# A four-layer graph kernel on one core: a low-bit check of the adjacency, a branch ahead of layer 3, and float32r halves behind it

## The chip, the core and the metric

The kernel runs on one core of a Trainium2 chip. Its metric is the device time in microseconds (us); lower is better. Three timed executions gave 1043.35, 1043.86 and 1045.03 us, so the median is 1043.86 us. One more execution was taken with the hardware profiler, and every row below comes from it.

Four engines of the core compute: TensorE (PE in the profile; its weight loads are PEld), VectorE (DVE), ScalarE (ACT) and GpSimd (POOL). The queues of SyncE (SP), ACT and POOL issue transfers.

## The reference, cut to what matters

The inputs are x (2708 nodes x 128 features), adj (2708 x 2708, zeros and ones with a full diagonal) and small weights. Four layers follow each other, each of the form x = x + layer(relu(layernorm(x))):

- Layer 0: attention over adj with a row sum.
- Layer 1: adj plus the identity, scaled on both sides by the root of its degrees, times the features, times a weight, relu.
- Layer 2: adj transposed times the features, divided by degrees, two weights, a batch norm over all nodes, relu.
- Layer 3, where the change lies:

```python
XW = jnp.matmul(X, W)
s_col = jnp.matmul(XW, a[0, :f])
s_row = jnp.matmul(XW, a[0, f:])
Z1 = jax.nn.leaky_relu(s_row[:, None] + s_col[None, :], negative_slope=0.01)
den = jnp.exp(Z1)
num = jnp.matmul(A, den)
att = jnp.where(num != 0, den / jnp.where(num != 0, num, 1.0), 0.0)
H = jnp.matmul(A, jnp.matmul(att, XW))
```

A and den are both 2708 x 2708, so `num` alone would be a product of 2708 x 2708 x 2708.

## The kernel before, in words

The nodes are cut into T = 22 tiles of 128 (the last has 20 rows), and the 2708 columns of a result into NB = 6 blocks: five of 512 and one of 148 (`E0`). All operands of the large products are float32. A product (`product`, `aggregate`) streams one tile of adjacency rows (128 x 2708, 1354 KB) after the other from HBM, uses the tile as the moving operand for all six blocks, and sums into six PSUM accumulators; the last four tiles are taken block by block, so that each block can be finished (`finish1`, `finish2`, `finish3`) while the next is summed. In layer 2 the loads go through `load_with_turn`; three tiles of adj are kept in SBUF from layer 0 (`kept`), the others come through seven stream buffers.

Layer 3 avoids the cubic product. It ranks the nodes by their row score and cuts them into chunks of CH = 126 nodes in that order (`CH = P - 2`, `NC` = 22 chunks). The exponential of a leaky relu has two branches. For a column node, all chunks but one lie wholly on one branch, so their share of `num` is a sum that is formed once per chunk (`sums`, `wts`): two rows per chunk, kept in HBM as `pre_d`. Only the chunk in which the change of branch falls has to be multiplied out. The column nodes are sorted into NE = 22 steps of 128 such that each step needs at most two chunks (NS = 44 half steps). For a half step, `fetch` gathers the CH adjacency rows of the chunk into a tile of 128 rows by an indirect transfer on the POOL queue, and a second gather puts the two rows of `pre_d` into the partitions behind them. The matching stationary operand `dmat[:, s, :]` (128 x 128) is made by `densities`. Lines 933 to 941 move the finished chunk sums from PSUM through `hn` to `pre_d`.

The loop of layer 3 (lines 965 to 992) does, for each of the 22 steps s:

- the gathers of the two half steps (four buffers `rows`, in pool `steps`) and of the step's feature rows (`fetch_xw`), on POOL;
- `e` = max(row_a + c_rel, 0) on DVE (line 975);
- for each of six blocks a PSUM bank `num` that gets two products, one per half step (line 980), then its logarithm on ACT into `ln` (line 984). There are two such banks;
- three subtractions e - ln on DVE (line 986) and the exponential of the whole `e` on ACT (line 988). Each logarithm and exponential stage is preceded by a load of ACT's function table;
- `spread_values(s - 1)`: six products of the step before with its `e` as the moving operand (line 962), summed over all steps in six accumulators.

The products of the loop are pinned in the order in which they are written: the `num` products of step s, then the values of step s - 1, then the `num` products of step s + 1.

After the loop the accumulators are turned and scaled into `hn` (lines 997 to 1002), and a last product (lines 1026 to 1028) streams the 22 tiles of adj_t again through SP's queue, with `hn` as the stationary operand; the streaming buffers are the four of `steps` and three of `late`. `finish3` turns a finished block, adds it to x and stores it.

Of the kernel before, what the change touches and what calls it, by code (L numbers as in the profile page):

```python
# [8 lines left out]
F32 = mybir.dt.float32  # L9
BF16 = mybir.dt.bfloat16  # L10
I32 = mybir.dt.int32
AF = mybir.ActivationFunctionType
# [5 lines left out]
def kernel(  # L18
# [19 lines left out]
    nc = tc.nc  # L38
# [23 lines left out]
    def fill(a, src, t):  # L62

        if rows(t) < P:
            nc.gpsimd.memset(a, 0.0)
        nc.sync.dma_start(a[: rows(t), :], src[t * P : t * P + rows(t), :])
        return a
# [138 lines left out]
    def aggregate(stationary, moving, accs, start, stop, blocks=range(NB)):  # L206
        for b in blocks:
            lo, hi = E0[b]
            nc.tensor.matmul(accs[b][:, : hi - lo], stationary, moving[:, lo:hi], start=start, stop=stop)  # L209
# [13 lines left out]
    with ExitStack() as stack:  # L223
# [168 lines left out]

        def load_with_turn(t):
            a = kept[t] if t in kept else load_rows(adj, t)
            if t not in kept and turns:
                b = turns.pop(0)
                p = bank()
                turned(p, h2, TILES[b])
                nc.vector.tensor_copy(hT[:, spans(b)], p[:, : len(TILES[b]) * P])
            return a  # L400
# [11 lines left out]
        product(order2, lambda t: h2[:, t, :], load_with_turn, range(NB), finish2)  # L412
        nc.vector.bn_aggr(tot[:, 0:2], st2)
# [15 lines left out]
    CH = P - 2  # L429
# [6 lines left out]
    pre_d = dram.tile([2 * NC, N], F32, name="pre_d")  # L436
# [4 lines left out]
    def stream_rows(src, t):  # L441
        pool = pools[0]
        pools.append(pools.pop(0))
        return fill(pool.tile([P, N], F32, tag="rows", name="rows"), src, t)
# [9 lines left out]
    r_exp = keepers.tile([P, T], F32, name="r_exp")  # L454

    def gather(out, src, idx):
# [5 lines left out]
        )  # L462

# [3 lines left out]
    with tc.tile_pool(name="tab", bufs=1) as tab, tc.tile_pool(name="tabs", bufs=2) as tabs:  # L467
# [27 lines left out]
        nc.vector.memset(first[0:1, :], 1.0)  # L495
        slope_hi = const.tile([P, 1], F32, name="slope_hi")
        nc.vector.tensor_scalar(slope_hi, part, float(CH), -0.99, ALU.is_equal, ALU.mult)
        nc.vector.tensor_scalar_add(slope_hi, slope_hi, 1.0)
        slope_lo = const.tile([P, 1], F32, name="slope_lo")
        nc.vector.tensor_scalar(slope_lo, part, float(CH + 1), 0.99, ALU.is_equal, ALU.mult)  # L500
        nc.vector.tensor_scalar_add(slope_lo, slope_lo, 0.01)
# [425 lines left out]
        for s0 in range(0, FIRST, 4):  # L927
            densities(s0)
        for t in range(NEARLY, T):
            sums(t)  # L930
        for s0 in range(FIRST, NS, 4):
            densities(s0)
        pre_sb = hn.rearrange("p t d -> p (t d)")[:, : 3 * BW].rearrange("p (b i) -> p b i", i=BW)
        with tc.high_priority():
            for b in range(3):
                w = BLK[b][1] - BLK[b][0]
                nc.scalar.copy(pre_sb[: 2 * NC, b, :w], accs[b][: 2 * NC, :w])
                nc.vector.tensor_copy(pre_sb[64 : 64 + 2 * NC, b, :w], accs[b][64 : 64 + 2 * NC, :w])
            flat = hn.rearrange("p t d -> p (t d)")
            for h, queue in enumerate((nc.sync, nc.scalar)):  # L940
                queue.dma_start(pre_d[:, h * HALF : (h + 1) * HALF], flat[64 * h : 64 * h + 2 * NC, :HALF])

    with tc.tile_pool(name="att", bufs=2) as attp:

        accs = [acc_bank(b) for b in range(NB)]
        done = {}

        def fetch(s):
            if s < 2:
                a = first_rows[s][:, :N]  # L950
            else:
                a = steps.tile([P, N], F32, tag="rows", name="rows")
                one = gather(a[:CH, :], adj_t[:, :], row_i[:CH, s : s + 1])
                if s < 6:
                    tc.keep_in_program_order(one)
            gather(a[CH:, :], pre_d[:, :], pre_i[0:2, s : s + 1])
            return a
# [7 lines left out]
        for s in range(NE):  # L965
            a2 = [fetch(2 * s + h) for h in range(2)]
            if s >= 3:
                fetch_xw(s)
            xw = xw_s[s % 4]
            m = nc.vector.tensor_scalar_mul(xw, xw, c_exp[:, s : s + 1])  # L970
            if s < 4:
                tc.keep_in_program_order(m)
            e = attp.tile([P, N], F32, tag="e", name="e")
            ln = attp.tile([P, N], F32, tag="ln", name="ln")
            nc.vector.tensor_scalar(e, row_a[:, :N], c_rel[:, s : s + 1], 0.0, ALU.add, ALU.max)  # L975
            beg = 0
            for b, (lo, hi) in enumerate(E0):
                num = bank()
                for h in range(2):
                    m = nc.tensor.matmul(  # L980
                        num[:, : hi - lo], dmat[:, 2 * s + h, :], a2[h][:, lo:hi], start=(h == 0), stop=(h == 1)
                    )
                    tc.keep_in_program_order(m)
                nc.scalar.activation(ln[:, lo:hi], num[:, : hi - lo], AF.Ln, bias=tiny)  # L984
                if b in (2, 4, 5):
                    nc.vector.tensor_sub(e[:, beg:hi], e[:, beg:hi], ln[:, beg:hi])  # L986
                    beg = hi
            nc.scalar.activation(e, e, AF.Exp)
            done[s] = (xw, e)
            if s:  # L990
                spread_values(s - 1)
        spread_values(NE - 1)


    scale = small.tile([P, T], F32, tag="scale", name="scale")
    nc.vector.scalar_tensor_tensor(scale, deg, 0.0, r_exp, ALU.not_equal, ALU.mult)
    for b in range(NB):
        evacuate(b, yT, accs[b])
        p = bank()
        turned(p, yT, TILES[b], True)  # L1000
        for q, t in enumerate(TILES[b]):
            nc.vector.tensor_scalar_mul(hn[:, t, :], p[:, cols(q)], scale[:, t : t + 1])


    late = ctx.enter_context(tc.tile_pool(name="late", bufs=3))
    pools = [steps] * 4 + [late] * 3

    def finish3(b, acc):
        evacuate(b, yT, acc)
        p = bank()  # L1010
        turned(p, yT, TILES[b], True)
        t0 = TILES[b][0]
        f = len([t for t in TILES[b] if t < TF])
        nc.vector.tensor_add(
            xs[:, t0 : t0 + f, :].rearrange("p t d -> p (t d)"),
            xs[:, t0 : t0 + f, :].rearrange("p t d -> p (t d)"),
            p[:, : f * P],
        )
        nc.sync.dma_start(
            out[t0 * P : (t0 + f) * P, :].rearrange("(t p) d -> p t d", p=P), xs[:, t0 : t0 + f, :]  # L1020
        )
        if f < len(TILES[b]):
            nc.vector.tensor_add(xs[:TAIL, TF, :], xs[:TAIL, TF, :], p[:TAIL, cols(f)])
            nc.sync.dma_start(out[TF * P :, :], xs[:TAIL, TF, :])

    product(
        list(range(T)), lambda t: hn[:, t, :], lambda t: stream_rows(adj_t, t), range(NB), finish3
    )
# [32 lines left out]
```

## Time and profile before

| what | value |
|---|---|
| median of three timed executions | 1043.86 us |
| the profiled execution: its own time | 1046.11 us |
| the profiled execution: span | 1044.3 us |
| PE busy, share of the span | 956.5 us, 92% |
| DVE, ACT, POOL busy | 461.3, 440.4, 165.3 us |
| mean granted TensorE clock | 0.972 |
| first product of the layer 3 loop to last product of the kernel | 613.7 to 1039.0 us |
| bytes moved | 213.06 MB, mean 204 GB/s |

How to read it: a float32 product on 128 columns of weights shows as two MATMUL records (and two weight loads). A group's row gives the line, the engine, the operation, the tiles written and read, the count, the busy time and the mean duration of one. Matmuls are pipelined: durations of neighbours overlap, so the pace is read from the busy time of a run of them. The idle time in a row is that of the engine just before the group, with what ended it. The profiled execution took 1.8 us more than its span and 2.25 us more than the median.

### The profile page before, as it was taken

How to read it: one execution, taken by the hardware profiler on the slowest of the kernel's cores; microseconds unless marked ns; L12 is line 12 of the kernel's file. 1: busy time of each engine (PE TensorE's matmuls, PEld its weight loads, DVE VectorE, ACT ScalarE, POOL GpSimd, SP SyncE). 2: the span in 40 equal slices, each digit the busy share in tenths (PEclk: the TensorE clock that was granted, in tenths of full speed). 3: DMA queues.
4: the chain of work that ended last, by engine and by line, in shares of the span. 5: the costliest groups of instructions: out<-in, count | busy, mean ns of one | idle time of the engine just before them, and what ended most of it. 6: DMA issues, size and time to landing. Idle time of an engine off the chain costs nothing.

```text
span 1044.3 us, 8022 instructions
## 1 busy us (share of the span) xinstructions
PE 956.5 (92%) x2850; PEld 426.0 (41%) x2850; DVE 461.3 (44%) x869; ACT 440.4 (42%) x579; POOL 165.3 (16%) x156
## 2 busy tenths in 40 slices
PE   4699999999999999966697768999999999999998
PEld 3333333344454544442232123444444444444444
DVE  5799889660004100269787242333333333340002
ACT  4579775230005000168402665665656666640000
POOL 3000001020002000020002041444334443200000
PEclk9899999999999999988899889999999999999999
DMA  8257445258865683074069744655556655569841
GB/s 300 94 213 266 175 165 192 55 225 310 309 229 205 221 302 123 0 320 162 1 257 360 198 163 177 218 192 187 183 200 218 216 181 193 198 249 369 312 170 53
DMA packets 36426, 213.06 MB, mean 204 GB/s; under 512 B 8043, under 2 KB 16923, under 8 KB 17363
## 3 DMA queue, kind: packets, MB, share of 16 engines
q1 hardware_dynamic: 21223, 146.96, 38.0%
q0 software_dynamic: 9152, 62.46, 17.0%
q10 hardware_dynamic: 6011, 3.14, 1.2%
q8 instruction: 22, 0.36, 0.1%
q14 instruction: 18, 0.14, 0.0%
HBM read 209.23 MB, written 3.32 MB: 204 GB/s over the span
## 4 chain that ended last, share of the span: by engine, by line
PE 77%; DVE 9%; ACT 7%; DMA 3%; issue 2%; POOL 1%; ACTq 0%; DVEq 0%; POOLq 0%
PE acc L209 37%; PE bank L980 16%; PE acc L962 10%; PE bank L301 7%; ACT L984 3%; DMA rows<-in_adj_t_dram 2%; PE acc L640 2%; ACT ln L984 1%; POOL rstd L160 1%; DVE bits L577 1%; PE bank L185 1%; DVE st L171 1%; ACT row_a L580 1%; PE bank L917 1%; PE acc L252 1%
## 5 line engine op out<-in xcount | busy, mean ns | idle before, releaser
L980 PE MATMUL bank<-rows,dflat 128*128 128x512 f32 x504 | 201.7, 550 | 10.6 <-ACT ln L984 10.6
L980 PEld LDWEIGHTS bank<-rows,dflat 128*128 128x128 f32 x504 | 90.6, 191 | 119.7 <-issue 91.5
L986 DVE TENSOR_TENSOR e<-e,ln 128x1536 f32<-128x1536 f32 (+2 forms) x66 | 70.5, 1097 | 145.3 <-ACT ln L984 145.3
L984 ACT ACTIVATE ln<-bank,tiny 128x512 f32<-128x512 f32 x132 | 79.4, 634 | 83.4 <-PE bank L980 83.2
L962 PE MATMUL acc<-e,xw 128*128 128x512 f32 (+1 forms) x264 | 103.4, 542 | 0.0
L209 PE MATMUL acc<-rows,hn 128*128 128x512 f32 (+1 forms) x264 | 101.7, 542 | 0.0
L209 PE MATMUL acc<-a,hn 128*128 128x512 f32 (+1 forms) x264 | 100.9, 542 | 0.0
L209 PE MATMUL acc<-a,hs 128*128 128x512 f32 (+1 forms) x228 | 88.1, 542 | 0.0
L286 ACT ACTIVATE tau<-row_a,e_neg,e_lo 128x1536 f32<-128x1536 f32 (+1 forms) x44 | 65.0, 1509 | 37.3 <-PE bank L301 27.4
L204 ACT COPY yT<-acc 128x512 f32<-128x512 f32 x9 | 5.2, 581 | 178.4 <-PE acc L209 174.9
L301 PE MATMUL bank<-tau,pick 128*6 128x512 f32 x180 | 72.6, 542 | 0.0
L962 PEld LDWEIGHTS acc<-e,xw 128*128 128x128 f32 x264 | 48.7, 190 | 52.6 <-issue 47.6
L209 PEld LDWEIGHTS acc<-a,hn 128*128 128x128 f32 x264 | 47.0, 190 | 50.2 <-issue 50.0
L209 PEld LDWEIGHTS acc<-rows,hn 128*128 128x128 f32 x264 | 46.8, 190 | 49.0 <-issue 48.8
L457 POOL DMA_INDIRECT rows<-in_adj_t_dram,row_i x42 | 41.9, 998 | 154.2 <-PE bank L980 147.8
L209 PE MATMUL acc<-yT,hs 128*128 128x512 f32 x132 | 57.6, 574 | 7.8 <-DVE yT L292 7.8
L289 DVE SCALAR_TENSOR_TENSOR tau<-tau,e_hi,a 128x1536 f32<-128x1536 f32 (+1 forms) x38 | 60.5, 1623 | 3.0 <-ACT tau L286 3.0
L975 DVE TENSOR_SCALAR e<-row_a,c_rel 128x2708 f32<-128x2708 f32 x22 | 35.8, 1630 | 57.3 <-PE acc L962 57.2
L209 PEld LDWEIGHTS acc<-a,hs 128*128 128x128 f32 x228 | 41.2, 190 | 45.4 <-issue 45.4
L640 PE MATMUL acc<-rows,wts 128*44 128x452 f32 (+1 forms) x216 | 49.3, 568 | 9.5 <-DMA rows<-in_adj_t_dram 9.4
L457 POOL DMA_INDIRECT xw<-xw_d,xw_i x22 | 41.2, 1873 | 93.7 <-DVE xw_i L841 87.3
L209 PE MATMUL acc<-row_b,hs 128*128 128x512 f32 x132 | 55.5, 553 | 0.0
(343 smaller groups left out, 1048.9 us busy)
## 6 DMA issues: line engine op xcount, KB each, us to landing
a<-in_adj_dram SPq DMA_DIRECT2D x38, 1354.0 KB, 6.5
rows<-in_adj_t_dram SPq DMA_DIRECT2D x38, 1354.0 KB, 7.2
a<-in_adj_t_dram SPq DMA_DIRECT2D x21, 1354.0 KB, 5.8
keep<-in_adj_dram SPq DMA_DIRECT2D x2, 1354.0 KB, 5.8
dflat<-in_adj_t_dram SPq DMA_DIRECT2D x2, 1354.0 KB
xw_d<-hs ACTq DMA_DIRECT2D x1, 1408.0 KB
row_a<-rdeg_d ACTq DMA_DIRECT2D x1, 1354.0 KB
yT<-in_adj_t_dram SPq DMA_DIRECT2D x1, 1354.0 KB, 5.6
```

The costliest lines, as they stand in the source:

```text
L160: nc.gpsimd.tensor_tensor(dst, s[:, :n], neg_half[:, :n], ALU.pow)
L209: nc.tensor.matmul(accs[b][:, : hi - lo], stationary, moving[:, lo:hi], start=start, stop=stop)
L286: nc.scalar.activation(tau[:, :w], row_a[:, h0:h1], AF.Relu, bias=e_neg[:, t : t + 1], scale=e_lo[:, t : t + 1])
L289: nc.vector.scalar_tensor_tensor(tau[:, :w], tau[:, :w], e_hi[:, t : t + 1], a[:, h0:h1], ALU.add, ALU.mult)
L301: nc.tensor.matmul(den[: len(E0), : hi - lo], pick[:, b, :], tau[:, lo - h0 : hi - h0], start=(ndone == 0), stop=(t == T - 1 and b == NB - 1),
L457: return nc.gpsimd.indirect_dma_start(out=out, out_offset=None, in_=src, in_offset=bass.IndirectOffsetOnAxis(ap=idx, axis=0),)
L640: nc.tensor.matmul(accs[b][64 * h : 64 * h + 2 * NC, : hi - lo], wts[:, t, :], a[:, lo:hi], start=(t == 0), stop=(t == T - 1),)
L962: m = nc.tensor.matmul(accs[b][:, : hi - lo], xw, e[:, lo:hi], start=(s == 0), stop=(s == NE - 1))
L975: nc.vector.tensor_scalar(e, row_a[:, :N], c_rel[:, s : s + 1], 0.0, ALU.add, ALU.max)
L980: m = nc.tensor.matmul(num[:, : hi - lo], dmat[:, 2 * s + h, :], a2[h][:, lo:hi], start=(h == 0), stop=(h == 1))
L984: nc.scalar.activation(ln[:, lo:hi], num[:, : hi - lo], AF.Ln, bias=tiny)
L986: nc.vector.tensor_sub(e[:, beg:hi], e[:, beg:hi], ln[:, beg:hi])
```

## The change

The change reads the adjacency once for its low bits, sets a flag, and puts the layer 3 loop and the last product behind a branch on that flag. If any adjacency entry has a bit among its twelve lowest, the old float32 arithmetic runs (`rest(False, ...)`). Otherwise `rest(True, ...)` runs, in which the adjacency tiles and gathered rows are of type float32r, and the other operand of each product is cut into a high and a low float32r half, each of which is multiplied once with the tile.

- Layer 2: for each of the 22 adj tiles, DVE masks the low twelve bits into `yT` or `row_b` and ACT sums them into a column of `low`. The first checks wait until the fourth streamed tile; then up to two are made per loaded tile.
- Ahead of the layer 3 loop: `low` is reduced, summed by a 1 x 1 product and compared; the result is the integer `flag`. The chunk size goes from 126 to 124 nodes (22 chunks still), because each gathered tile now takes four rows of `pre_d`: the two sums, cut into high and low halves. `pre_d` has 88 rows instead of 44, written by four transfers instead of two, after a mask and a subtraction per block on DVE.
- The gathers of the first four half steps (steps 0 and 1) stay ahead of the branch and in float32; steps 0 and 1 use the old products.
- In the exact arm, steps 2 to 21 gather into float32r tiles, DVE makes `d_hi` and `d_lo` from the step's two stationary operands, and each block has four products instead of two. `ln` has one buffer instead of two.
- After the loop, DVE makes `y_hi` and `y_lo` (128 x 22 x 128 each) from `hn`. The last product streams float32r tiles, and `fill` issues these loads on POOL's queue instead of SP's. `late` has one buffer instead of three.
- The transfers into float32r tiles read float32 from HBM, so they change the type on the way.

```diff
     def fill(a, src, t):
         if rows(t) < P:
-            nc.gpsimd.memset(a, 0.0)
-        nc.sync.dma_start(a[: rows(t), :], src[t * P : t * P + rows(t), :])
+            nc.gpsimd.memset(a if a.dtype == F32 else a.bitcast(F32), 0.0)
+        queue = nc.sync if a.dtype == F32 else nc.gpsimd
+        queue.dma_start(a[: rows(t), :], src[t * P : t * P + rows(t), :])
...
     def aggregate(stationary, moving, accs, start, stop, blocks=range(NB)):
+        parts = stationary if isinstance(stationary, list) else [stationary]
         for b in blocks:
             lo, hi = E0[b]
-            nc.tensor.matmul(accs[b][:, : hi - lo], stationary, moving[:, lo:hi], start=start, stop=stop)
+            for i, w in enumerate(parts):
+                nc.tensor.matmul(accs[b][:, : hi - lo], w, moving[:, lo:hi],
+                    start=start and i == 0, stop=stop and i == len(parts) - 1)
...
+        low = const.tile([P, T], F32, name="low")
+        nc.gpsimd.memset(low, 0.0)
+        unchecked = []
+        def low_bits(t, a):
+            junk = (yT, row_b)[t % 2][:, :N]
+            bits = junk.bitcast(I32)
+            m = nc.vector.tensor_scalar(bits, a.bitcast(I32), 0xFFF, None, ALU.bitwise_and)
+            n = nc.scalar.activation(junk, bits, AF.Identity, accum_out=low[:, t : t + 1])
...
         def load_with_turn(t):
             a = kept[t] if t in kept else load_rows(adj, t)
+            unchecked.append((t, a))
+            if 3 <= t < TF - 2 or t == TF:
+                for _ in range(min(2, len(unchecked))):
+                    low_bits(*unchecked.pop(0))
...
-    CH = P - 2
+    CH = P - 4
...
-    pre_d = dram.tile([2 * NC, N], F32, name="pre_d")
+    pre_d = dram.tile([4 * NC, N], F32, name="pre_d")
...
+    def high_bits(dst, src):
+        nc.vector.tensor_scalar(dst.bitcast(I32), src.bitcast(I32), -4096, None, ALU.bitwise_and)
...
+        low_all = tab.tile([P, 1], F32, name="low_all")
+        nc.vector.tensor_reduce(low_all, low, AX.X, ALU.add)
+        p = acc_bank(4)
+        nc.tensor.matmul(p[:1, :1], low_all, ones[:, 0:1], start=True, stop=True)
+        flag_f = tab.tile([1, 1], F32, name="flag_f")
+        nc.vector.tensor_scalar(flag_f, p[:1, :1], 0.0, None, ALU.is_gt)
+        nc.vector.tensor_copy(flag, flag_f)
...
             for b in range(3):
...
+                high_bits(pre_hi[:w, lo:hi], flat[:w, lo:hi])
+                nc.vector.tensor_sub(pre_lo[:w, lo:hi], flat[:w, lo:hi], pre_hi[:w, lo:hi])
+            for o, part_sb in ((0, pre_hi), (2 * NC, pre_lo)):
+                for h, queue in enumerate((nc.sync, nc.scalar)):
+                    queue.dma_start(
+                        pre_d[o : o + 2 * NC, h * HALF : (h + 1) * HALF], part_sb[64 * h : 64 * h + 2 * NC, :HALF]
+                    )
...
+    for s in range(4):
+        ahead[s] = fetch(s)
+    def rest(exact, stack3):
...
+            for s in range(NE):
+                short = exact and s >= 2
+                a2 = [rows_of.pop(2 * s + h, None) or fetch(2 * s + h, F32R if short else F32) for h in range(2)]
...
+                if short:
+                    d_hi = attp.tile([P, 2, P], F32R, tag="d_hi", name="d_hi")
+                    d_lo = attp.tile([P, 2, P], F32R, tag="d_lo", name="d_lo")
+                    nc.vector.tensor_copy(d_hi, d2)
+                    nc.vector.tensor_sub(d_lo, d2, d_hi)
+                    terms = [(d[:, h, :], a2[h]) for h in range(2) for d in (d_hi, d_lo)]
+                else:
+                    terms = [(d2[:, h, :], a2[h]) for h in range(2)]
...
+                    for i, (d, a) in enumerate(terms):
+                        m = nc.tensor.matmul(
+                            num[:, : hi - lo], d, a[:, lo:hi], start=(i == 0), stop=(i == len(terms) - 1)
+                        )
...
+            if exact:
+                ts = slice(TILES[b][0], TILES[b][-1] + 1)
+                nc.vector.tensor_copy(y_hi[:, ts, :], hn[:, ts, :])
+                nc.vector.tensor_sub(y_lo[:, ts, :], hn[:, ts, :], y_hi[:, ts, :])
...
+        with tc.tile_pool(name="late", bufs=1 if exact else 3) as late:
+            pools[:] = [steps] * 4 + [late] * (1 if exact else 3)
+            product(list(range(T)), y_of, lambda t: stream_rows(adj_t, t, F32R if exact else F32), range(NB), finish3)
+
+    some_low = nc.values_load(flag[0:1, 0:1], min_val=0, max_val=1, skip_runtime_bounds_check_because="0 or 1")
+    with tc.If(some_low > 0) as general:
+        with ExitStack() as s3:
+            rest(False, s3)
+    with general.Else():
+        with ExitStack() as s3:
+            rest(True, s3)
```

## The prediction

> **What bounds the kernel now.** I read the page first: busy times, queues, the chain that ended last and the costliest groups.
>
> ```profile
> PE 956.5 (92%) x2850; PEld 426.0 (41%) x2850; DVE 461.3 (44%) x869; ACT 440.4 (42%) x579; POOL 165.3 (16%) x156
> ...
> q1 hardware_dynamic: 21223, 146.96, 38.0%
> q0 software_dynamic: 9152, 62.46, 17.0%
> ...
> L980 PE MATMUL bank<-rows,dflat 128*128 128x512 f32 x504 | 201.7, 550 | 10.6 <-ACT ln L984 10.6
> L962 PE MATMUL acc<-e,xw 128*128 128x512 f32 (+1 forms) x264 | 103.4, 542 | 0.0
> L209 PE MATMUL acc<-rows,hn 128*128 128x512 f32 (+1 forms) x264 | 101.7, 542 | 0.0
> ```
>
> TensorE is the bound. Lines 980 and 209 (rows,hn), which the change rewrites, hold 303 us of it; line 962 stays float32. The queues give the price of bytes: q0, the POOL queue's, moved 62.46 MB in 17.0% of 1044.3 us, so 352 GB/s while it worked; q1 the same way gives 370 GB/s.
>
> Next, the timeline of one step of the loop; the rows on either side repeat every 14.30 us.
>
> ```profile
> 739.18 4.71 PE L962 MATMUL acc<-e,xw 128*128 128x512 f32 x12
> ...
> 743.72 3.60 PE L980 MATMUL bank<-rows,dflat 128*128 128x512 f32 x8
> 743.92 1.63 DVE L975 TENSOR_SCALAR e<-row_a,c_rel 128x2708 f32<-128x2708 f32 x1 [2.88 <-PE acc L962]
> ...
> 744.33 2.06 POOL L457 DMA_INDIRECT xw<-xw_d,xw_i  x1 [0.30 <-issue]
> ...
> 745.68 1.28 ACT L984 ACT_TABLE_LOAD   x1 [2.07 <-PE bank L980]
> ...
> 746.98 1.27 ACT L984 ACTIVATE ln<-bank,tiny 128x512 f32<-128x512 f32 x2
> ...
> 747.72 5.92 PE L980 MATMUL bank<-rows,dflat 128*128 128x512 f32 x16 [0.40 <-ACT ln L984]
> ```
>
> PE runs values 4.54 us, then two blocks (eight records), then waits 0.40 us for the first logarithm, which stood behind a 1.28 us table load that began only when block 0 was there. Then come the other four blocks. ACT needs 3.8 (logarithms) + 2.46 (exponential) + 2 x 1.28 = 8.8 us a step.
>
> The stretches of one step and of the last product, by engine, clock, DMA share and GB/s:
>
> ```profile
> 656.35:670.65 14.30, 13.90 (x37) 6.37 (x36) 4.84 (x4) 8.63 (x10) 5.78 (x6) 1.00 0.57 197
> 930.00:945.00 15.00, 14.99 (x55) 8.05 (x54) 7.80 (x25) 1.76 (x3) 0.00 (x0) 1.00 0.84 342
> 945.00:1018.00 73.00, 73.00 (x194) 34.49 (x194) 0.00 (x0) 0.00 (x0) 2.35 (x1) 1.00 0.74 273
> ```
>
> PE is full in both; transfers use 0.57 to 0.74 of the engines, and with free buffers they reach 342 GB/s. So transfers are the next bound. Last, PE's pace, from the bfloat16 products of the ranking, and the hand-over to the loop:
>
> ```profile
> 500.56 1.19 PE L586 MATMUL acc<-bits,pick_b 128*6 128x512 bf16 x5 [1.07 <-DVE bits L577]
> 502.83 1.24 PE L586 MATMUL acc<-bits,pick_b 128*6 128x512 bf16 x5 [1.03 <-DVE bits L577]
> ...
> 606.38 0.30 ACTq L941 DMA_DIRECT2D pre_d<-hn  x1
> ...
> 610.56 0.87 POOL L457 DMA_INDIRECT hT<-pre_d,pre_i  x1 [28.07 <-DMA pre_d<-hn]
> ...
> 613.70 2.04 PE L980 MATMUL bank<-hT,dflat 128*128 128x512 f32 x2 [6.14 <-DMA hT<-pre_d,pre_i]
> ```
>
> From one bfloat16 row to the next 128 columns are added for 0.05 us: 0.4 ns a column. Twelve float32 records cover 2 x 2708 columns in 4.54 us: 0.84 ns a column. A float32 product is two records of two column times each.
>
> **The change part by part**, against the profiled 1046.11 us (2.25 above the median); the sum is then taken off the median.
>
> *Layer 2 check: 0.* Each tile costs one DVE mask (as line 975, 1.63 us) and one ACT sum (line 274 has the same shape at 2.45, plus 0.19 to read the accumulator). 22 x 2.64 = 58 us on ACT. From 365 to 420 us ACT is idle and DVE has 1.1 us of work, while PE takes 4.55 us a tile from seven buffers. What waits behind the last check is `finish2`'s work on `yT` and `row_b`; should the last two checks run late it costs 2 x 2.64 = 5 us. I keep 0, bounds 0 and 5.
>
> *Flag, masks of constants: 0.* Some tenths on DVE beside the transfer wait of 22 us in `sums` (575 to 598 us); at most 1.
>
> *Hand-over of the chunk sums: +3.5.* Between 604.16 and 606.34 us DVE made three copies; three masks (452 of 2708 columns of 1.63, so 0.33 each) and three subtractions (0.69 for 512, so 0.62) follow serially: 2.9. The second transfer on each queue adds 0.3 of issue and as much of landing. PE already waits here, so all of it counts. Bounds 2.5 and 5.
>
> *Branch: +1.* The sequencers read the flag and jump past the other arm. No branch is in the trace; the longest unexplained issue gap on the chain is 2.90 us. PE has 6 us (now nearly 10) of waiting to hide it in, POOL jumps after its gathers of steps 0 and 1. Bounds 0 and 6 (two gaps, nothing hidden). Gathers 4 and 5, issued ahead of it before, are first needed some 30 us later.
>
> *Loop steps 2 to 21: -69.* What a float32r record costs is not in the trace: between the bfloat16 pace (0.42 ns a column) and the float32 record's (0.84). The float32 record spends its second column time on the moving operand's low part; a 12-bit operand has none, so I take the lower. The Trainium skill, "FP8 and Floating Point Precision", TensorE Precision Notes, says that true float32 takes four passes and that a reduced form truncates to FP22. No row here shows that form; by that page alone I would put the six blocks at an estimated 4.5 us.
>
> Then a 512 block takes four records, 0.86 us, not 1.71. The small block takes four records that are bound by weight loads (0.19 us each), 0.7. Step from the end of values: block 0 done at 0.86, first logarithm through at 0.86 + 0.17 (signal) + 1.28 + 0.69 + 0.15 = 3.15 (before 4.00); block 1 is done at 1.7, so PE idles 1.4 where it idled 0.40: the table load is late next. Blocks 2 to 5 follow at the alternation of two banks until 6.3, values 4.54: 10.85 us instead of 14.30. The exponential of the step ends as values end (last logarithm, 1.45 us of subtractions, 2.46), so ACT just fits. DVE gets `d_hi`, `d_lo` (0.35 + 0.4); they could stand behind `e`, which waits for values, and would then delay every step by 1.63 + 0.75 = 2.4, or 48 us in all; but their inputs are ready a step earlier, so I take 0.
>
> The transfers must keep up: a step moves 2.84 MB; at 352 GB/s 8.1 us. POOL issues for 2 x (0.97 + 0.88) + 2.06 + five gaps of 0.30 = 7.3 us. Both fit 10.85, but the type-changing form of these transfers has no row. Its rate lies between 352 and, as I put the lower end, half of it, 176: the rate of the step window above is 197. I take 352, because packets and bytes are the same.
>
> Against the change speaks the Trainium skill, "SBUF — State Buffer", SBUF: two separate sides: a DVE copy in two-port mode locks GpSimd out, so a POOL-issued transfer cannot write its descriptors. The trace agrees: the `xw` gather beside line 975 takes 2.06 us, its shortest 0.94. By that rule the new copies add an estimated 0.35 us a step to POOL, inside its 3.5 us of slack.
>
> *Last product: -20.* The queue moves from SP to POOL, whose only other work here is the memset (2.35 us), and buffers go from seven to five. With E for the end of values: first product at E+5.5 before; the DVE split of the first block (0.35 + 0.69) and its signals make E+7.5. The five buffers are full by then. A tile takes PE 2.45 us (4.55 before), so tile 0's buffer is free at E+10. Tiles 5 to 20 follow at 1.387 MB / 352 = 3.94 us, after 2 us of latency: E+75; the short tile with its memset E+78. The remaining blocks (1.73 + 0.6 of turning each) take 11, and the end 5.3 as now (1039.0 to 1044.3): E+94 against E+114.6 (values end at 929.7). The product becomes bound by transfers, not PE (22 x 2.45 = 54).
>
> Sum: 3.5 + 1 - 69 - 20 = -84.5; 1043.86 - 84.5 = 959, said as 960.
>
> **The rivals.** For a transfer rate r in MB/us a step takes 2.84/r once this exceeds 10.85, and the last product ends at E + 12 + 16 x 1.387/r + 19.
>
> - *Middling transfers* (r 0.215 to 0.264). At 0.24: steps 11.8, -50; product E+123.5, +9; with +4.5 about 1007. A doubled POOL cost of the gathers (7.3 to 13 us a step) lands near there too.
> - *Slow type-changing transfers* make it slower: the mechanism is the rate of POOL-queue transfers into float32r tiles in loop and last product. It decides below 0.215, 61% of the measured 352: steps 13.2, -22; product +20; +4.5. At 0.176: steps 16.1, +37; product +43; sum +84, 1128. For it: every byte of both stages takes this path, and there are now five buffers instead of seven. Against: the gathers' 0.97 us and 352 GB/s carry over if only the element changes.
> - *float32r takes two column times*: then halves mean as much PE time as before; loop 0, product +2, with +4.5 some 1050. The change would not do what it says.
> - *The flag is set* and the old arm runs: +4.5, 1048. Against: one and zero have no low bits.
>
> **How the numbers follow.** Forecast (fast transfers) 0.50, own range 940 to 985: 20 x 1 us either way in the step, late `d_lo`, 5 us in the hand-over. Middling 0.14, slow transfers 0.23, two column times 0.09, flag 0.04. Faster by over 0.2% (2.1 us, about what a measurement here can tell) is 0.62, taking the first two with a little for no change at the crossing; same 0.02; slower 0.36. The range 940 to 1080 takes in the middling case, 1048 and 1050, and slow transfers down to r = 0.19; 0.15 lies above it, 0.05 below.
>
> **What would show it.** Right: a step of about 10.9 us, line 980's successor with 480 records in the 20 steps at about 0.22 us pace, ACT table loads waiting as now, DMA share above 0.7 in the loop, PE in the last product waiting on DMA rows. Wrong: steps of 13 us or more in which PE waits for DMA rows, or POOL busy end to end; records of 0.43 us; an unchanged count on the old arm; PE waiting for DVE `d_lo`; a gap over 12 us ahead of the loop.

## The result and the profile after

The changed kernel takes 1524.63 us (median of 4 runs, 1510.99 to 1533.21), the kernel before 1044.44 us on the same chip (1043.35 to 1047.39). The ratio is 1.458, with a 95% interval of 1.446 to 1.470. The forecast was 960 us, range 940 to 1080: wrong in sign and far outside the range.

The profiled execution took 1521.11 us, its span is 1519.3 us. Page of the changed kernel: busy times, the granted clock in 40 slices, DMA engines, rates, queues, and two of the costliest groups (busy, mean ns | idle before, releaser):

```profile
PE 906.4 (60%) x2852; PEld 457.8 (30%) x2852; DVE 518.3 (34%) x956; ACT 495.1 (33%) x623; POOL 191.0 (13%) x179
...
PEclk9899999999998898776666666666666666666988
DMA  7275438754626097253333333333333433333885
GB/s 270 107 259 181 149 147 289 269 216 197 242 109 222 5 369 179 61 124 64 77 76 79 76 77 76 75 75 75 75 75 75 75 75 75 75 73 74 299 310 201
...
q0 software_dynamic: 27712, 91.86, 24.8%
...
L1051 PE MATMUL bank<-rows,d_hi 128*128 128x512 f32 x240 | 125.5, 527 | 471.3 <-DMA rows<-pre_d,pre_i 458.3
...
L489 POOL DMA_INDIRECT rows<-in_adj_t_dram,row_i x42 | 58.3, 1389 | 559.3 <-PE bank L1051 552.3
```

PE does 50 us less work than before (906.4 against 956.5), as intended, and then stands still: it waits 458 us for gathered rows in front of line 1051. The loop fills the slices from the 18th on, at 73 to 79 GB/s for the most part, with the DMA engines 0.3 to 0.4 busy and the clock at 0.6 to 0.7. Nothing there is at its limit: not PE, not POOL (13%), not the engines' bytes. Something is late. A step of 13 us or more in which PE waits for DMA rows is the first sign of being wrong that the prediction itself named.

What is late stands in the view of DMA issues, whose last column is the median from issue to landing. First the kernel before, then the changed one:

```profile
rows<-in_adj_t_dram,row_i POOLq DMA_INDIRECT x42, 8.5
rows<-pre_d,pre_i POOLq DMA_INDIRECT x42, 7.4
```

```profile
rows<-in_adj_t_dram SPq DMA_DIRECT2D x17, 1354.0 KB, 16.2
...
rows<-in_adj_t_dram,row_i POOLq DMA_INDIRECT x42, 26.5
rows<-pre_d,pre_i POOLq DMA_INDIRECT x42, 24.8
```

A gather lands 26.5 us after its issue, three times as late. The timeline of one loop step of the changed kernel shows when it is issued:

```profile
1067.44 4.75 PE L1022 MATMUL acc<-e,xw 128*128 128x512 f32 x12
...
1068.61 1.74 POOL L489 DMA_INDIRECT rows<-in_adj_t_dram,row_i  x1 [29.20 <-PE bank L1051]
...
1074.59 0.88 POOL L489 DMA_INDIRECT rows<-pre_d,pre_i  x1 [0.30 <-issue]
...
1094.65 0.77 PE L1051 MATMUL bank<-rows,d_hi 128*128 128x512 f32 x1 [22.46 <-DMA rows<-pre_d,pre_i]
...
1097.96 0.77 PE L1051 MATMUL bank<-rows,d_hi 128*128 128x512 f32 x1 [2.12 <-DMA rows<-pre_d,pre_i]
...
1104.94 1.28 POOL L489 DMA_INDIRECT rows<-in_adj_t_dram,row_i  x1 [28.21 <-PE bank L1051]
```

POOL waits 29 us for the products of one step to free their two buffers, then gathers into them, and PE's very next products need just these rows. From 1068.61 the four gathers take 6 us to issue, the last lands 23.4 us later, the products take 6.7 us: 36 us, and the next step's first gather goes out at 1104.94. Before, the step was 14.30 us. So two things are wrong at once: the landing is late, and the gathers run one step ahead of PE, not two.

Why one step, the POOL timeline after the hand-over shows:

```profile
632.66 3.02 POOL L489 DMA_INDIRECT rows<-in_adj_t_dram,row_i  x1 [0.30 <-issue]
...
642.89 2.54 POOL L489 DMA_INDIRECT rows<-in_adj_t_dram,row_i  x1 [0.30 <-issue]
645.73 0.88 POOL L489 DMA_INDIRECT rows<-pre_d,pre_i  x1 [0.30 <-issue]
661.12 0.98 POOL L489 DMA_INDIRECT xw<-xw_d,xw_i  x1 [14.51 <-DMA rows<-in_adj_t_dram,row_i]
679.77 0.96 POOL L489 DMA_INDIRECT xw<-xw_d,xw_i  x1 [17.67 <-PE acc L1022]
698.70 1.30 POOL L489 DMA_INDIRECT rows<-in_adj_t_dram,row_i  x1 [17.97 <-PE bank L1051]
```

Halves 2 to 5 are gathered at 632.66 to 645.73 into the four `steps` buffers. Halves 2 and 3 (step 1) go into tiles made ahead of the branch. Step 1's products end before the values of step 0 start at 674.79, yet half 6 is not gathered until 698.70, when step 2's products are done. The two buffers of step 1 are not taken again inside the arm.

The stages, from start to the loop's first product, from there to the end of the values (E, where the next product of PE starts: 934.2, 1413.8 and 896.0 us), and from E to the end of the span. In the kernel before, the last two sets of values follow each other, 24 records in one row:

```profile
925.04 9.29 PE L962 MATMUL acc<-e,xw 128*128 128x512 f32 x24
934.17 1.04 PE L185 MATMUL bank<-ident,yT 128*128 128x128 f32 x8
```

The prediction put E at 929.7, the end of the first of these two sets. So its E+114.6 is E+110.1. Its difference of -20 is hardly touched, since it counted the old and the new product from the same place.

| | before | forecast | changed | rows split, gathers 2 and 3 in the arm |
|---|---|---|---|---|
| to first loop product | 613.7 | +4.5 | 634.3 (+20.6) | 622.4 (+8.8) |
| loop | 320.5 | -69 | 779.5 (+459.1) | 273.6 (-46.9) |
| after E | 110.1 | -20 | 105.5 (-4.6) | 76.3 (-33.8) |
| span | 1044.3 | | 1519.3 | 972.3 |

The last column is an experiment below: the whole change with two repairs.

### The profile page after: what moved, and what is told of

It reads as the page before. It is cut to its first block, busy times and chain, and to the rows that moved or that the text cites. A ratio compares the mean times of both kernels' runs of the same rounds, so it can differ in the third digit from the quotient of the medians.

```text
span 1519.3 us, 8240 instructions
## 1 busy us (share of the span) xinstructions
PE 906.4 (60%) x2852; PEld 457.8 (30%) x2852; DVE 518.3 (34%) x956; ACT 495.1 (33%) x623; POOL 191.0 (13%) x179
## 3 DMA queue, kind: packets, MB, share of 16 engines
q0 software_dynamic: 27712, 91.86, 24.8%
## 4 chain that ended last, share of the span: by engine, by line
DMA 41%; PE 38%; DVE 7%; POOL 5%; issue 4%; ACT 4%; SPq 0%; POOLq 0%; ACTq 0%; DVEq 0%
DMA rows<-pre_d,pre_i 31%; PE acc L213 20%; PE bank L1051 7%; DMA rows<-in_adj_t_dram 6%; PE bank L311 5%; POOL rows L489 4%; DMA rows<-in_adj_t_dram,row_i 2%; ACT L1055 2%; PE acc L680 2%; DMA xw<-xw_d,xw_i 2%; POOL rstd L162 1%; PE acc L1022 1%; ACT ln L1055 1%; DVE bits L617 1%; DVE st L173 1%
## 5 line engine op out<-in xcount | busy, mean ns | idle before, releaser
L1051 PE MATMUL bank<-rows,d_hi 128*128 128x512 f32 x240 | 125.5, 527 | 471.3 <-DMA rows<-pre_d,pre_i 458.3
L1051 PEld LDWEIGHTS bank<-rows,d_hi 128*128 128x128 f32 x240 | 60.9, 254 | 520.3 <-issue 429.8
L1041 DVE TENSOR_SCALAR xw<-xw,c_exp 128x128 f32<-128x128 f32 x22 | 6.3, 285 | 438.2 <-DMA xw<-xw_d,xw_i 437.3
L489 POOL DMA_INDIRECT rows<-in_adj_t_dram,row_i x42 | 58.3, 1389 | 559.3 <-PE bank L1051 552.3
L1051 PE MATMUL bank<-rows,d_lo 128*128 128x512 f32 x240 | 113.3, 481 | 0.0
L213 PE MATMUL acc<-rows,y_hi 128*128 128x512 f32 x132 | 54.3, 419 | 27.5 <-DMA rows<-in_adj_t_dram 27.5
L1051 PEld LDWEIGHTS bank<-rows,d_lo 128*128 128x128 f32 x240 | 62.2, 259 | 9.1
L680 PE MATMUL acc<-rows,wts 128*44 128x452 f32 (+1 forms) x216 | 51.4, 594 | 20.4 <-DMA rows<-in_adj_t_dram 20.4
L1059 ACT ACTIVATE e<-e 128x2708 f32<-128x2708 f32 x22 | 54.1, 2460 | 11.6 <-DVE e L1057 11.3
## 6 DMA issues: line engine op xcount, KB each, us to landing
rows<-in_adj_t_dram SPq DMA_DIRECT2D x17, 1354.0 KB, 16.2
```

The costliest lines, as they stand in the source:

```text
L213: nc.tensor.matmul(accs[b][:, : hi - lo], w, moving[:, lo:hi], start=start and i == 0, stop=stop and i == len(parts) - 1,)
L489: return nc.gpsimd.indirect_dma_start(out=out, out_offset=None, in_=src, in_offset=bass.IndirectOffsetOnAxis(ap=idx, axis=0),)
L680: nc.tensor.matmul(accs[b][64 * h : 64 * h + 2 * NC, : hi - lo], wts[:, t, :], a[:, lo:hi], start=(t == 0), stop=(t == T - 1),)
L1051: m = nc.tensor.matmul(num[:, : hi - lo], d, a[:, lo:hi], start=(i == 0), stop=(i == len(terms) - 1))
```

## The theories

- **R, rows of a gather.** The number of rows in a gather decides how many DMA engines serve it: the largest number up to 16 that divides the rows. 126 rows are spread over 14 engines, 9 each; 124 rows (the change's `CH = P - 4`) over 4 engines, 31 each.
- **H, held buffers.** Tiles made ahead of the branch stay taken until both arms join. Two of four `steps` buffers hold halves 2 and 3, so the loop cycles through two.
- **T, the type change** of the transfers into float32r tiles makes them slow: the forecast's own rival.

The source of R is the Trainium skill, "DMA: Bandwidth & Descriptors", "Why a DMA increments its semaphore by 16 and not by 1": it states the divisor rule, gives 100 partitions on 10 engines and 127 on one as examples, and names an exception for some direct copies from GpSimd's queue. The landings of 8.5 and 26.5 us agree with it. No view names the engines of a gather, but how many are busy can be read. Here are a stretch of the kernel before, then one of the changed kernel (after the times: busy us of PE, PEld, DVE, ACT, POOL, then clock, DMA share, GB/s):

```profile
741.50:749.50 8.00, 7.60 (x19) 3.23 (x19) 1.83 (x2) 4.66 (x4) 3.98 (x4) 1.00 0.86 321
```

```profile
1078.00:1092.00 14.00, 0.00 (x0) 0.00 (x0) 0.00 (x0) 0.00 (x0) 0.00 (x0) 0.50 0.53 123
```

With gathers of 126 rows the DMA share is 0.86, and 14 of 16 would be 0.88. With two gathers of 124 rows on their way it is 0.53, and 8 of 16, four for each, would be 0.50. The trace's packet records agree: mostly 14 row packets are under way at a time in the first stretch, mostly 8 or 9 in the second.

## The experiments

**1. The kernel before, with chunks of 124 rows.** Float32, no branch, no halves.

```diff
-    CH = P - 2
+    CH = 124
+    K = CH + 2
...
-gather(a[CH:, :], pre_d[:, :], pre_i[0:2, s : s + 1])
+gather(a[CH:K, :], pre_d[:, :], pre_i[0:2, s : s + 1])
```

The numerator's products run on 126 partitions (`dmat[:K]`, `a2[h][:K]`).

> The kernel before with one size changed: chunks of 124 nodes instead of 126, the two sums behind them, products over 126 partitions; all float32, no branch, four buffers. Theory R (the number of rows of a gather decides how long it takes: 124 rows land in some 25 us, 126 in 8.5, whatever the type): the two gathers of a step issued at the end of its products land 26 to 29 us later, two steps ahead, so a step takes about (29 + 9.7) / 2 = 19 to 23 us instead of 14.3, and the two early gathers slow the streamed tiles of the chunk sums by some 15 us; 1150 to 1260 us in all. Theory T (the change of type makes the transfers slow) and theory H alone (two of the four buffers are held across the branch): 1044 us within 1%.

Measured: 1234.46 us, ratio 1.179 (1.174 to 1.184). Its queue, DMA issues and a window of the loop:

```profile
q0 software_dynamic: 24640, 61.57, 23.9%
...
rows<-in_adj_t_dram,row_i POOLq DMA_INDIRECT x42, 28.8
```

```profile
770.00:1110.00 340.00, 257.66 (x549) 111.85 (x550) 77.14 (x76) 133.68 (x138) 78.46 (x71) 0.82 0.62 131
```

Two rows fewer in a gather, and the landing goes from 8.5 to 28.8 us: 31 rows for 9 are 3.4 times as many, and the landing is 3.4 times as long. The step averages 21.8 us. Neither T nor H exists in this kernel. The packets of the queue went from 9,152 to 24,640, for 1.4% fewer bytes.

**2. The changed kernel, each gather cut into 112 and 12 rows** (16 engines with 7, 12 with 1, by R). `row_j` is a copy of the last indices, since a gather's indices start at partition 0.

```diff
-            one = gather(a[:CH, :], adj_t[:, :], row_i[:CH, s : s + 1])
-            if s < 6:
-                tc.keep_in_program_order(one)
+            for r0, r1, idx in ((0, 112, row_i), (112, CH, row_j)):
+                one = gather(a[r0:r1, :], adj_t[:, :], idx[: r1 - r0, s : s + 1])
+                if s < 6:
+                    tc.keep_in_program_order(one)
```

> The changed kernel with each gather of 124 rows made as two, of 112 and of 12 rows; branch, types and buffers as they are. R with H: landing falls from 25 to about 8 us, but the gathers of the next step are still issued only when the products of this one end, so a step is 6.3 us of products plus 12 to 15 us until the last rows are there: 18 to 21 us, and 1120 to 1190 us in all. R without H: steps of about 10.9 us, 960 to 990 us. T: steps stay above 30 us, near 1500 us.

Measured: 1201.03 us, ratio 1.152 (1.146 to 1.158); steps of 21.3 to 23.9 us where 18 to 21 were expected, and a time 11 us above the expected range. 324 us are gone by the form of the gather alone. PE still waits in every step, because the gathers are issued when the step's products end and needed right after: H is left.

**3. The changed kernel, gathers 2 and 3 moved into the arms.** The rows stay in gathers of 124.

```diff
-    for s in range(4):
+    for s in range(2):
         ahead[s] = fetch(s)
```

> The changed kernel with gathers 2 and 3 moved from ahead of the branch into its arms, so that no tile of the four-buffer pool is made outside; gathers of 124 rows as they are. H: two steps of gathers are in flight again, a step takes 18 to 22 us instead of 37, the last product has five buffers instead of three; 1150 to 1220 us. Without H (R or T alone): within 1% of the changed kernel's 1524 us.

Measured: 1163.01 us, ratio 1.108 (1.098 to 1.118). Landings are as late as before the repair (27.2 us), but there are two steps to hide them in: a step takes 16 to 24 us, not 37. The POOL timeline shows the buffers of step 1 taken again as soon as its products end, at 678.51 us, with the values of step 0 starting at 678.30:

```profile
678.51 1.29 POOL L489 DMA_INDIRECT rows<-in_adj_t_dram,row_i  x1 [28.95 <-PE bank L1051]
```

One number in a loop ahead of the branch was worth 362 us, 29 of them in the last product (E+76.8, not E+105.5).

**4. Both together.**

> Both edits: gathers of 112 and 12 rows, and gathers 2 and 3 inside the arms. R and H together are the whole loss: steps of 10.9 us bound by TensorE, the last product bound by its loads, 955 to 985 us, faster than the kernel before. If T has a share: steps above 13 us and over 1020 us.

Measured: 972.26 us, ratio 0.9295 (0.9265 to 0.9325): faster than both kernels, in the expected range, though its steps of 12.0 us are longer than the expected 10.9. Its queue, and windows in the loop, in the last product and, for comparison, in layer 2, whose loads keep their type:

```profile
q0 software_dynamic: 12224, 91.79, 36.9%
```

```profile
670.00:880.00 210.00, 178.19 (x624) 104.57 (x622) 98.17 (x122) 150.05 (x155) 126.49 (x120) 1.00 1.09 234
905.00:945.00 40.00, 36.74 (x168) 29.61 (x166) 2.72 (x9) 0.00 (x0) 7.56 (x14) 1.00 1.05 424
365.00:389.00 24.00, 24.00 (x67) 11.61 (x66) 16.05 (x11) 24.00 (x21) 0.00 (x0) 1.00 1.01 424
```

R and H are each worth over 300 us alone and overlap: with one repaired, the other's cost is 191 (1163.0 - 972.3) or 229 us (1201.0 - 972.3). T falls as the cause: the last product's type-changing loads run at 424 GB/s, the rate of the loads without it. The 552 us between this kernel and the changed one are R's and H's, and the type change is in both.

**5. The kernel before, its gather of 126 rows made as 64 and 62.** R says that these two smaller gathers are worse than the one (62 rows go on 2 engines, 31 each); anything to do with chunk size, partitions or bytes says that nothing happens. `row_j` lies in the constant `first`, which is free by then.

```diff
-                one = gather(a[:CH, :], adj_t[:, :], row_i[:CH, s : s + 1])
+                for r0, r1, idx in ((0, 64, row_i), (64, CH, row_j)):
+                    one = gather(a[r0:r1, :], adj_t[:, :], idx[: r1 - r0, s : s + 1])
```

> The kernel before, chunks of 126 as they were, only the gather of 126 rows made as two, of 64 and of 62 rows. Nothing else changes: same rows, bytes, float32, no branch. Theory R (the largest divisor up to 16 of the number of rows decides how many engines serve a gather: 64 rows go to 16 engines with 4 rows each, 62 rows to 2 with 31 rows each): the landing of the gathers rises from 8.5 us to some 29 or more, as 31 rows an engine did with 124 rows (28.8 us), and since two gathers a step then need two engines each, a step takes at least the 21.7 us of the 124-row run: 1,200 us or more, up to 1,900 if the same two engines serve them all. Rival theory S (it is the change of the chunk size, the four partitions of pre_d or the smaller share of bytes in a gather that made the 124-row run slow): smaller gathers land no later than 8.5 us, POOL issues two more instructions of 0.97 us a step beside 3.5 us of slack, and the time stays within 1,044 to 1,060 us.

Measured: 1239.74 us in one run, against 1041.1 to 1048.2 for the kernel before. Page and a loop window, then a loop window of the kernel before:

```profile
q0 software_dynamic: 28160, 62.54, 22.0%
...
L984 PE MATMUL bank<-rows,dflat 128*128 128x512 f32 x504 | 247.3, 648 | 143.5 <-DMA rows<-pre_d,pre_i 128.0
```

```profile
700.00:760.00 60.00, 42.54 (x95) 18.55 (x94) 13.81 (x12) 21.40 (x23) 20.41 (x18) 0.83 0.53 125
```

```profile
700.00:900.00 200.00, 194.41 (x505) 89.14 (x504) 70.46 (x70) 120.66 (x127) 80.74 (x70) 1.00 0.56 199
```

A rate of 125 GB/s where the same rows in one gather had 199, and PE waits 128 us for rows where it waited for none. It is the divisor of the row count that decides; this is the sharpest of the runs for R. That a gather is cut in two does not cost this by itself: the float32 run of section 6, cut into 112 and 12, takes 1059 us.

The packets of POOL's queue say the same, and exactly. Suppose a gather counts 16 packets for each row that one of its engines gets, and 16 more: 16 x 9 + 16 = 160 with 126 rows, 16 x 31 + 16 = 512 with 124, 80 + 512 with 64 and 62. Over 44 half steps run 1 then has 44 x (512 - 160) = 15,488 packets more than the kernel before, and this run 44 x (80 + 512 - 160) = 19,008 more. The pages have 24,640 - 9,152 = 15,488 and 28,160 - 9,152 = 19,008. That comes out if all 16 engines count as many packets as the ones that carry rows. (In section 6, a cut at 120 instead of 112 should add 44 x 16 = 704; it adds 12,928 - 12,224 = 704.)

**6. What keeps the repaired loop at 12 us a step.** In run 4 the loop's DMA share is 1.09 at 234 GB/s, in the kernel before 0.56 at 199. Four runs ask why a byte is dearer. The first is the float32 arm alone with the split gathers and no branch (`rest(False, s3)` in place of the branch):

> The changed kernel with its float32 arm alone and no branch, gathers as 112 and 12 rows. All transfers keep their type. PE bounds the loop again at 14.3 us a step, so about 1,048 us (1,040 to 1,065; ln has one buffer). What it is for is the price of a byte in the loop. In the kernel before, the loop's engines were 0.56 busy at 199 GB/s (355 for full), in the changed arithmetic with these split gathers 1.09 at 234 (215 for full). Theory C (the type change on gathers takes the engines' time): here, in float32, share to rate is as before, 0.52 to 0.62 at 195 to 200 GB/s. Rival theory D (the form with 112, 12 and 4 rows costs the engines more, whatever the type): 0.8 or more at the same rate.

The second is run 4 with the loop's gathers kept in float32 (into `hT`, `row_b`, `yT` and `hn`, which are free there) and cut to float32r by DVE:

```diff
-            a = steps.tile([P, N], kind, tag="rows", name="rows")
+            raws = [f[:, :N] for f in first_rows] + [yT[:, :N], hn.rearrange("p t d -> p (t d)")[:, :N]]
+            a = steps.tile([P, N], F32, tag="rows", name="rows") if kind == F32 else raws[s % 4]
...
+                    raw, a2 = a2, []
+                    for a in raw:
+                        a2.append(steps.tile([P, N], F32R, tag="rows", name="rows"))
+                        nc.vector.tensor_copy(a2[-1], a)
```

> The kernel with split gathers inside the arm (972 us), but the gathers of steps 2 to 21 keep float32, into four tiles that are free by then, and DVE copies each into a float32r tile (two of 2708 columns a step, 1.63 us each). Under theory C (the type change on gathers takes the engines' time) the loop's DMA share falls from 1.09 to about 0.65 at the same rate and PE no longer waits for gathered rows; the step is then 10.9 to 12.5 us, set by DVE's copies ahead of the products: 940 to 975 us. Under theory D (the form of the gathers costs) the share stays at 1.0 or more, PE still waits for rows, and the step is no shorter than 12.5 us: 972 to 1,000 us.

Measured: 1059.11 us (one run) and 1044.08 us (ratio 0.9991, 0.9973 to 1.0009). A loop window of the first, then one of the second and the second's wait on PE:

```profile
700.00:760.00 60.00, 58.12 (x152) 26.49 (x150) 21.59 (x22) 35.66 (x37) 32.47 (x30) 1.00 0.82 200
```

```profile
760.00:820.00 60.00, 47.37 (x142) 28.83 (x141) 33.16 (x33) 33.09 (x36) 36.35 (x28) 0.83 0.72 186
```

```profile
763.74 1.57 DVE L1045 CAST rows<-hn 128x2708 fp32r<-128x2708 f32 x1
...
765.36 0.50 PE L1060 MATMUL bank<-rows,d_hi 128*128 128x512 f32 x1 [2.75 <-DVE rows L1045]
```

Share and rate give what the engines would move at a share of 1: 355 GB/s before, 244 and 258 with split float32 gathers (200 / 0.82, 186 / 0.72), 215 with split float32r gathers (234 / 1.09). So a byte is dearer by some 40% in the split form (355 / 250), whatever the type, and perhaps by another sixth with the type change (250 / 215); theory D holds more of it than C. A share of 1.09 cannot be engines in use: the view adds up the times of packets that overlap. So this compares packet times, and how far a busy engine is a loaded one it does not say. The second run's time missed under both theories: its casts stand in DVE's queue, the second one behind `e` (line 1055), which itself waits for values, so PE waits for DVE and a step takes 14.7 to 16.0 us.

The last two keep run 4 and move the cut (to 64, to 120):

> As the kernel with gathers of 112 and 12 rows inside the arm (972 us, loop step 12.5 us, DMA share 1.09 at 234 GB/s), but cut as 64 and 60 rows: 64 rows go to 16 engines, 60 to 15, four rows each. If uneven pieces (12 and 4 rows) are what makes a byte dearer there than in the kernel before (215 to 250 GB/s for a full share against 355), the share falls to 0.9 or less, PE stops waiting for rows and the step nears 11 us: 940 to 955 us. If the price comes from having more engines in use at a time (all 16 instead of 14), or from the number of transfers, nothing changes: 968 to 976 us.

> The same with the cut at 120: 120 rows on 15 engines with eight rows each, and 4 rows on 4 engines. Theory R gives the same as 112 and 12: no engine has more than eight rows of one gather. If leaving an engine free, as the kernel before does with 126 rows on 14 engines, makes a byte cheaper, the share falls towards 0.8 and the step nears 11 us: 940 to 960 us. Otherwise 968 to 976 us. If eight rows on an engine instead of seven count by themselves, up to one seventh longer landings and 972 to 990 us.

Measured: 999.26 us (0.959, 0.956 to 0.961) with 64 and 60 rows, 1013.05 us (0.971, 0.968 to 0.974) with 120 and 4. Their loop windows, in that order:

```profile
760.00:820.00 60.00, 47.76 (x173) 28.65 (x172) 26.78 (x32) 39.60 (x45) 35.40 (x33) 1.00 1.11 221
```

```profile
760.00:820.00 60.00, 50.52 (x157) 30.09 (x155) 25.07 (x33) 38.33 (x39) 32.76 (x32) 0.89 1.05 207
```

Both are slower than 112 and 12 and than every range expected of them, and both rates are lower at about the same share. Even pieces are not the answer, nor is leaving an engine free. That a cut with a piece for all 16 engines and a small rest is best fits three points and is no more than that: why a gathered byte costs what it costs in pieces stays open.

**7. The price of the branch.** Run 4 with the exact arm alone.

```diff
-    with tc.If(some_low > 0) as general:
-        with ExitStack() as s3:
-            rest(False, s3)
-    with general.Else():
-        with ExitStack() as s3:
-            rest(True, s3)
+    with ExitStack() as s3:
+        rest(True, s3)
```

> The kernel with split gathers inside the arm (972 us), without the branch and without the float32 arm; the flag is still made. What the branch costs by itself: my forecast said 1 us (0 to 6). If it holds, 966 to 972 us. If the branch also stops loads or work of the arm from starting early (a wall between the stages), it is more: 955 to 966 us.

Measured: 972.33 us (969.98 to 975.69) against 972.26 with it: no difference that can be told, some 3 us either way. The loop's first product starts at 623.05 us without the branch and 622.45 with it. The branch costs nothing by itself; what it cost was the two buffers.

## Why the prediction was wrong

**The step that failed first: "I take 352, because packets and bytes are the same."** The bytes were: the POOL queue's 91.86 MB are 62.5 without the last product's 29.3, against 62.46. The packets were not: they rose from 9,152 to 24,640, not counting the 3,072 of the last product's loads (27,712 in all; 3,072 = 12,224 - 9,152). A gather that had 14 engines had 4, it landed in 26.5 us and not 8.5, and the rate in the loop was 76 GB/s. The edit behind it, 126 rows to 124, stood in the change as `CH = P - 4`, and the prediction costed the masks and subtractions that came with it, not the number itself. The lower end, 176, came from a window in which PE was the bound; it was no bound from below. In the prediction's formula a step of 2.84 MB at 0.076 MB/us takes 37.4 us, but that is no test of it: 76 GB/s is the step's bytes over the step's time. The formula has the transfers run without pause, while the step on the timeline is 29 us of gathers on their way (1068.61 to 1097.96) and 7 us of products, one after the other. The rival "slow type-changing transfers" had the sign but the wrong mechanism: run 1 is slow without a type change, and run 4 is fast with one.

**The second: "Gathers 4 and 5, issued ahead of it before, are first needed some 30 us later", and "buffers go from seven to five".** The gathers' order around the branch was costed, the life of their buffers was not. In the loop the depth fell from two steps to one (run 3: 362 us with late landings; runs 2 and 4: 229 us with early ones), and the last product had three buffers, E+105.5; with five, in run 4, it took E+76.3.

**Steps that held.** Layer 2's check is hidden: its last product ends at 445.5 us against 444.1, inside the 0 to 5 given. float32r takes one column time a record: 0.23 us from record to record at full clock (lines of 1055 in run 4), against a forecast of 0.22. The flag did not send the kernel to the old arm (240 records on `d_hi` and 240 on `d_lo`). The branch is 0, forecast 1. The logarithm's table load is late next, as said. On the rule of the Trainium skill weighed there ("SBUF — State Buffer", SBUF: two separate sides), POOL's issue beside DVE's copies, the trace agrees again: in run 4 a gather issued beside line 1050 takes 1.92 us, one issued elsewhere 1.04.

**Sizes that were off**, read from run 4, where the mechanism runs undisturbed. Its first steps on the timeline:

```profile
657.47 4.75 PE L1026 MATMUL acc<-e,xw 128*128 128x512 f32 x12
...
663.25 1.28 ACT L1059 ACT_TABLE_LOAD   x1 [1.25 <-PE bank L1055]
...
668.70 4.75 PE L1026 MATMUL acc<-e,xw 128*128 128x512 f32 x12
```

- The step: 10.85 forecast, 11.23 here (668.70 - 657.47), as long as rows are there. Later steps take 11.3 to 12.8 us; the mean of the 20 is 12.0, near the 11.8 that the rival "middling transfers" had for 240 GB/s. In the 20 exact steps PE waits 11.3 us for rows and 23.7 us for the first logarithm (1.2 a step, where 1.4 was forecast). A step of 12.55 us shows how a short wait grows:

```profile
766.89 0.94 POOL L490 DMA_INDIRECT rows<-in_adj_t_dram,row_i  x1 [0.30 <-issue]
...
769.19 0.48 PE L1055 MATMUL bank<-rows,d_hi 128*128 128x512 f32 x1 [1.08 <-DMA rows<-pre_d,pre_i]
...
769.99 1.28 ACT L1059 ACT_TABLE_LOAD   x1 [2.56 <-PE bank L1055]
...
772.02 0.50 PE L1055 MATMUL bank<-rows,d_hi 128*128 128x512 f32 x1 [1.19 <-ACT ln L1059]
```

  The second half's rows are late inside block 0, the table load can only follow block 0, and PE waits for ACT as well. That is -46.9 for the loop instead of -69: 20 steps shorter by 2.3 us in the mean (14.3 - 12.0) in place of 3.45, and 1 us gained at its ends.
- The last product: -33.8 instead of -20. The loads run at 424 GB/s, not 352: 3.27 us a tile for 3.94, 11 us over 17 tiles.
- The hand-over with the branch: +8.8 instead of +4.5 (+9.4 without the branch, section 7; why it is more than 4.5 stays open); PE waits 12.90 us ahead of the first loop product, where it waited 6.14. In the changed kernel it is +20.6: the first two gathers of 124 rows (47.8 us to land, 18.0 before) run beside the tiles that the chunk sums stream, which land in 16.2 us (7.2 in the median of all loads of that line before), and PE waits 20.4 us for them instead of 9.4. With the split gathers of run 4 it waits 10.2. Run 1, without the branch, starts its loop as late as the changed kernel, at 634.0 us. (The prediction's 0.33 us a mask is 0.27 by its own proportion, 0.2 in the sum.)

With these sizes the forecast's own case is 972 us, inside its 940 to 985, in part by luck: the loop gained 22 us less than forecast and the last product 14 us more. The change as planned existed; the change as written was a different one in two numbers: 124 and 4.

## What to carry to other kernels

When a change alters the number of rows of a gather, write down how many engines it can be spread over before costing its bytes: here 126 to 124 rows, 2% less, made landings three times as long, and 112 + 12 undid most of it. When a branch is put into a pipelined loop, follow every buffer that is taken ahead of it: a tile made ahead of the branch takes its buffer out of the rotation inside it, and a depth of two steps becomes one. A rate read where another engine is the bound is no lower bound for the transfers, least of all for ones whose shape changes.

## What the runs showed of the hardware

- A gather's landing followed the rows per engine that the divisor rule gives: 9 rows 8.5 us, 31 rows 28.8 us. The same rule turned a split into two smaller gathers (64 and 62) into a loss of 194 us (1239.7 against 1045.8).
- Gathers with few engines also move more packets for the same bytes: under 512 B 8,043 in the kernel before, 23,618 with 124 rows, 27,114 with 64 and 62. The queue's counts come out to the packet if each of the 16 engines counts as many packets as an engine that carries rows; so the engines without rows count small packets in their place. What these are for, no view shows.
- Loads that turn float32 into float32r on the way ran at 424 GB/s with a DMA share of 1.05; loads that keep the type ran at 424 with 1.01.
- PE that had waited was slower for a while: in the step shown, the granted clock is 0.50 from 1078 us on, in the wait, and still until 1101.20, and the records there follow each other in 0.43 us; from 1101.30 they take 0.23. Over the 8 records in between that is an estimated 1.6 us of a step of 37.

```profile
1094.60:1101.20 6.60, 4.09 (x8) 2.34 (x8) 0.29 (x1) 1.96 (x3) 0.00 (x0) 0.50 0.08 22
```
